# Layer 3's logits on four row groups, and layers 0 and 2 without fused weights

## The chip, the cores and the metric

The kernel runs on one core of a Trainium2 chip. A core has a matrix engine (TensorE, in the profile PE for its matmuls and PEld for its weight loads), a vector engine (VectorE, DVE), a scalar engine (ScalarE, ACT), a general engine (GpSimd, POOL), and queues that start transfers (SP's and ACT's among them). The metric is the device time of one execution in microseconds, lower being better. A profile of one execution gives each engine's instructions.

## The reference

Sixteen images of 256 channels on a 32 x 32 grid go through four layers; everything is float32. N is the 1024 grid places.

- Layer 0: group norm over 8 groups of 32 channels, then q, k and v by 256 x 256 matrices with biases, `softmax(q^T k / 16)` over 1024 places, the weighted sum of v, an output projection with bias, and the residual.
- Layer 1: mean and maximum over channels, two 3 x 3 convolutions on these maps, a sigmoid, and a product with the image.
- Layer 2: the same attention as layer 0 with other weights.
- Layer 3: attention without a norm, where q and k have only 32 rows:

```
energy = clip(q^T k * 32**-0.5, -10, 10)
out    = v softmax(energy)^T
x      = gamma * out + x
```

## The kernel before, in words

An image lies in the on-chip memory as 128 partitions x 2 channel chunks x 1024 places (`xt`). The constants are `CC` = 2 chunks, `HW` = 1024, `HALF` = 512, `NH` = 2 halves, `NT` = 8 tiles of 128 places, `DQK` = 32.

Before the first image `fuse` (lines 125 to 170) multiplies layer 0's q and k weights into one matrix, and its v and projection weights into another, so that logits are `(W xn)^T xn` and the value product gives the projected result at once; the biases are fused too. Layer 2's fuse is called in the first image's turn (line 442).

`attend` (lines 228 to 298) does layers 0 and 2. `group_norm` makes `xn`: statistics on VectorE, two small TensorE products with `gmat` (lines 181 and 189), the inverse root on GpSimd (line 193), scaling on VectorE (line 201). Then q (line 238, 8 products), `values` (line 214, 16 products of 256 columns), and for each half four row tiles: logits over all 1024 places into a two-bank PSUM tile (line 259), the row maximum on VectorE (267), exponential with row sum on ScalarE (270), reciprocal and scaling on VectorE (272, 273), eight transposes on TensorE (278), and their copies (281, 283). The value products follow (line 288), two groups of eight, each added into `xt` on VectorE (295).

`clipped_attend` (lines 365 to 433) does layer 3. One product per half gives q and k together (line 374: 64 output rows); q goes through VectorE (381), k through ScalarE (384). `values` follows. For each half, four pairs of key tiles: two logits products with 32 contraction rows (line 398) into a two-bank tile of `ps_s`, clip on VectorE (402), exponential in place on ScalarE (403). GpSimd adds the probability tiles (406 to 408), the value products run on TensorE (413), `ones` times the sums gives the denominators (423), VectorE takes the reciprocal (425), scales, adds the image (428, 429), and SP stores (432).

PSUM is in three pools, each with two buffers: `ps_s` (two banks a buffer: all logits), `ps_mm` (one bank: all other products) and `ps_tr` (one bank: transposes and denominators). There are three image buffers (`resp`).

Every `yield` ends a step. Two streams, even and odd images, alternate step by step, the second 8 steps behind (`OFFSET`). The tile framework's scheduler then may move instructions of one engine past each other; the order it settles on is fixed when the program is built, and each engine runs its own list in that order. Buffers are handed out in program order, and a writer waits for the last reader of its buffer.

Of the kernel before, what the change touches and what calls it, by code (L numbers as in the profile page):

```python
# [8 lines left out]
FP = mybir.dt.float32  # L9
AF = mybir.ActivationFunctionType  # L10
ALU = mybir.AluOpType
AX = mybir.AxisListType

P = 128
# [7 lines left out]
GROUP = 32  # L22
DQK = 32
EPS = 1e-5

# [10 lines left out]
def kernel(  # L36
# [39 lines left out]
    nc.scalar.dma_start(w0, w_l0.rearrange("(c p) o -> p c o", p=P))  # L76
    vb = const.tile([P, 1, C], FP, name="vb")
    nc.scalar.dma_start(vb[:, 0, :], v_bias[2:3, :].to_broadcast([P, C]))
    bv = const.tile([P, 2, CC], FP, name="bv")
    nc.scalar.dma_start(bv, v_bias[:2, :].rearrange("l (c p) -> p l c", p=P))  # L80
    sc = const.tile([P, NSCAL], FP, name="sc")
    nc.scalar.dma_start(sc, scal.to_broadcast([P, NSCAL]))
    qkb = const.tile([2 * DQK, 1], FP, name="qkb")
    nc.scalar.dma_start(qkb, qk_bias)
    w2 = const.tile([P, CC, 4 * C], FP, name="w2")
    nc.scalar.dma_start(w2, w_l2.rearrange("(c p) o -> p c o", p=P))
    w3 = const.tile([P, CC, 2 * DQK + C], FP, name="w3")
    nc.scalar.dma_start(w3, w_l3.rearrange("(c p) o -> p c o", p=P))

    ident = const.tile([P, P], FP, name="ident")  # L90
# [19 lines left out]
    def build_toep():  # L110
# [9 lines left out]
        nc.vector.tensor_scalar(neg_b2, sc[:, S_B2 : S_B2 + 1], -1.0, None, ALU.mult)  # L120

    def fuse(w, base, layer, nm):
        fw = const.tile([P, CC, 2 * C], FP, name=f"fw_{nm}")
        fb = const.tile([P, CC, 2], FP, name=f"fb_{nm}")
        nat = work.tile([P, CC, 3 * C], FP, tag="nat", name=f"nat_{nm}", bufs=1)
        for j in range(3):
            for r in range(CC):  # L130
                tr = ps_tr.tile([P, C], FP, tag="tr", name=f"wtr_{nm}_{j}_{r}")
                for c in range(CC):
                    nc.tensor.transpose(
                        tr[:, c * P : (c + 1) * P],
                        w[:, c, j * C + r * P : j * C + (r + 1) * P],
                        ident,
                    )
                nc.vector.tensor_copy(nat[:, r, j * C : (j + 1) * C], tr)
        for i in range(CC):
            ps = ps_mm.tile([P, HALF], FP, tag="mm", name=f"fw_{nm}_{i}")  # L140
            for j in range(2):
                lhs, src, rhs = (0, nat, C) if j == 0 else (2 * C, w, 3 * C)
                for r in range(CC):
                    nc.tensor.matmul(
                        ps[:, j * C : (j + 1) * C],
                        nat[:, r, lhs + i * P : lhs + (i + 1) * P],
                        src[:, r, rhs : rhs + C],
                        start=(r == 0),
                        stop=(r == CC - 1),
                    )  # L150

            nc.vector.tensor_scalar(fw[:, i, :C], ps[:, :C], C**-0.5, None, ALU.mult)
            nc.vector.tensor_copy(fw[:, i, C:], ps[:, C:])
        for i in range(CC):
            ps = ps_mm.tile([P, HALF], FP, tag="mm", name=f"fb_{nm}_{i}")
            for j in range(2):
                src, lhs = (nat, C) if j == 0 else (w, 3 * C)
                for r in range(CC):
                    nc.tensor.matmul(
                        ps[:, j : j + 1],  # L160
                        src[:, r, lhs + i * P : lhs + (i + 1) * P],
                        vec[:, r, base + 2 : base + 3] if j == 0 else bv[:, layer, r : r + 1],
                        start=(r == 0),
                        stop=(r == CC - 1),
                    )
            nc.vector.tensor_scalar(fb[:, i, 0:1], ps[:, 0:1], C**-0.5, None, ALU.mult)
            nc.vector.tensor_tensor(
                fb[:, i, 1:2], ps[:, 1:2], vec[:, i, base + 4 : base + 5], ALU.add
            )
        return fw, fb  # L170

# [34 lines left out]
    def values(src, w, col, bias, nm):  # L206

        vt = qkvp.tile([P, NT, C], FP, tag="vt", name=f"vt_{nm}")
        for t2 in range(NT // 2):
            ps = ps_mm.tile([P, 2, C], FP, tag="mm", name=f"vps_{nm}_{t2}")  # L210
            for i in range(2):
                t = 2 * t2 + i
                for c in range(CC):
                    nc.tensor.matmul(  # L214
                        ps[:, i, :],
                        src[:, c, t * P : (t + 1) * P],
                        w[:, c, col : col + C],
                        start=(c == 0),
                        stop=(c == CC - 1),
                    )  # L220
            dst = vt[:, 2 * t2 : 2 * t2 + 2, :]
            if bias is None:
                nc.vector.tensor_copy(dst, ps)
            else:
                nc.vector.tensor_tensor(dst, ps, bias.to_broadcast([P, 2, C]), ALU.add)
        return vt

    def attend(xt, w, fb, base, nm):

        xn = group_norm(xt, base, base + 1, nm)  # L230
        yield
        q = qkvp.tile([P, CC, HW], FP, tag="q", name=f"q_{nm}")
        for o in range(CC):
            for h in range(NH):
                hs = slice(h * HALF, (h + 1) * HALF)
                ps = ps_mm.tile([P, HALF], FP, tag="mm", name=f"q_{nm}_{o}_{h}")
                for c in range(CC):
                    nc.tensor.matmul(  # L238
                        ps,
                        w[:, c, o * P : (o + 1) * P],  # L240
                        xn[:, c, hs],
                        start=(c == 0),
                        stop=(c == CC - 1),
                    )
                nc.scalar.activation(q[:, o, hs], ps, AF.Identity, bias=fb[:, o, 0:1])
            yield
        vt = values(xn, w, C, None, nm)
        yield

        for h in range(NH):  # L250
            hs = slice(h * HALF, (h + 1) * HALF)
            pt = ptp.tile([P, NT, HALF], FP, tag="pt", name=f"pt_{nm}_{h}")
            for j in range(TPH):
                n0 = (h * TPH + j) * P
                s = ps_s.tile([P, HW], FP, tag="s", name=f"s_{nm}_{h}_{j}")
                for mh in range(NH):
                    ms = slice(mh * HALF, (mh + 1) * HALF)
                    for c in range(CC):
                        nc.tensor.matmul(  # L259
                            s[:, ms],  # L260
                            q[:, c, n0 : n0 + P],
                            xn[:, c, ms],
                            start=(c == 0),
# [10 lines left out]
                for g in range(2):  # L274
# [7 lines left out]
                    else:  # L282
                        nc.scalar.copy(dst, tr)  # L283
                yield
            for c in range(CC):
                ps = ps_mm.tile([P, HALF], FP, tag="mm", name=f"av_{nm}_{h}_{c}")
                for m in range(NT):
# [5 lines left out]
                        stop=(m == NT - 1),  # L293
                    )
                nc.vector.scalar_tensor_tensor(  # L295
                    xt[:, c, hs], ps, fb[:, c, 1:2], xt[:, c, hs], ALU.add, ALU.add
                )
                yield

# [65 lines left out]
    def clipped_attend(xt, b):  # L365


        q = qkvp.tile([DQK, HW], FP, tag="q", name=f"q3_{b}")
        k = qkvp.tile([DQK, HW], FP, tag="k", name=f"k3_{b}")
        for h in range(NH):  # L370
            hs = slice(h * HALF, (h + 1) * HALF)
            ps = ps_mm.tile([P, HALF], FP, tag="mm", name=f"qk3_{b}_{h}")
            for c in range(CC):
                nc.tensor.matmul(  # L374
                    ps[: 2 * DQK, :],
                    w3[:, c, : 2 * DQK],
                    xt[:, c, hs],
                    start=(c == 0),
                    stop=(c == CC - 1),
                )  # L380
            nc.vector.tensor_scalar(
                q[:, hs], ps[:DQK, :], qkb[:DQK], DQK**-0.5, ALU.add, ALU.mult
            )
            nc.scalar.activation(
                k[:, hs], ps[DQK : 2 * DQK, :], AF.Identity, bias=qkb[DQK : 2 * DQK]
            )
        vt = values(xt, w3, 2 * DQK, vb[:, 0:1, :], f"l3_{b}")
        yield

        for h in range(NH):  # L390
            hs = slice(h * HALF, (h + 1) * HALF)

            pt = ptp.tile([P, NT, HALF], FP, tag="pt", name=f"pt3_{b}_{h}")
            for m2 in range(NT // 2):
                s = ps_s.tile([P, 2, HALF], FP, tag="s", name=f"s3_{b}_{h}_{m2}")
                for i in range(2):
                    m = 2 * m2 + i
                    nc.tensor.matmul(  # L398
                        s[:, i, :], k[:, m * P : (m + 1) * P], q[:, hs], start=True, stop=True
                    )  # L400
                e = pt[:, 2 * m2 : 2 * m2 + 2, :]
                nc.vector.tensor_scalar(e, s, -10.0, 10.0, ALU.max, ALU.min)  # L402
                nc.scalar.activation(e, e, AF.Exp)  # L403
                yield
# [29 lines left out]

    fw0, fb0 = fuse(w0, L0_GAMMA, 0, "l0")
    late = []

    def sample(b, xt):
        yield from attend(xt, fw0, fb0, L0_GAMMA, f"l0_{b}")
        if b == 0:  # L440
            build_toep()
            late.extend(fuse(w2, L2_GAMMA, 1, "l2"))
        yield from spatial_gate(xt, f"l1_{b}")
        yield from attend(xt, *late, L2_GAMMA, f"l2_{b}")
        yield from clipped_attend(xt, b)
# [79 lines left out]
```

## Time and profile before

| what | us |
|---|---|
| median of 3 runs | 3787.77 |
| lowest and highest | 3785.66, 3788.89 |
| the profiled execution, its own time | 3787.77 |
| its span, first to last instruction | 3785.9 |
| TensorE busy in the span | 3625.0 |
| weight loads busy | 1831.1 |
| VectorE, ScalarE, GpSimd busy | 1661.3, 701.4, 309.4 |
| line 398 (layer 3 logits) busy, 512 records | 303.9 |

The mean granted TensorE clock is 0.957. In the profile's groups a line reads: line of the kernel, engine, operation, output tile <- input tiles, shapes, count, then busy time in us and mean ns of one, then the idle time of that engine just before, with what ended it. A matmul's own duration includes its passage through the array, so that durations in a sequence overlap; the distance between starts is what one costs in a stream. Digit rows cut the span into 40 slices, and each digit is tenths.

### The profile page before, as it was taken

The numbers are of one execution on the slowest core, as the hardware profiler recorded it, in microseconds if no ns is written. First come the engines' busy times: TensorE is split into PE (matmuls) and PEld (weight loads), VectorE is DVE, ScalarE is ACT, GpSimd is POOL, SyncE is SP. The second block draws the span as 40 slices with busy tenths as digits, with TensorE's granted clock in tenths as the row PEclk, the third lists the DMA queues.
The fourth block names the chain that finished last, engine by engine and source line by source line (L and its number), as shares of the span: only waits on it lengthen the run. The fifth ranks groups of instructions, "written<-read, shape, count | busy, mean of one in ns | idle before, by whom it ended". The sixth has DMA issues, their size and how long they took to land.

```text
span 3785.9 us, 26399 instructions
## 1 busy us (share of the span) xinstructions
PE 3625.0 (96%) x10808; PEld 1831.1 (48%) x10808; DVE 1661.3 (44%) x2544; ACT 701.4 (19%) x1073; POOL 309.4 (8%) x301
## 2 busy tenths in 40 slices
PE   7999899998999989999999999999999999999998
PEld 4554345543555435454455544555445554455543
DVE  5543435434344334453344533445334453344533
ACT  1112112121121111221112211212212121121211
POOL 0000100001000010000100001000110001100011
PEclk9999899998999989999899998999989999899998
DMA  1000000000000000000000000000000000000000
GB/s 63 1 1 0 23 23 0 1 0 22 23 1 1 0 23 23 1 0 6 17 23 1 1 6 20 20 0 0 6 23 17 1 1 6 23 6 0 1 6 17
DMA packets 15943, 38.01 MB, mean 10 GB/s; under 512 B 2512, under 2 KB 3024, under 8 KB 15824
## 3 DMA queue, kind: packets, MB, share of 16 engines
q1 hardware_dynamic: 13824, 33.56, 2.5%
q10 hardware_dynamic: 2000, 2.78, 0.2%
q8 instruction: 85, 1.39, 0.1%
q14 instruction: 34, 0.28, 0.0%
HBM read 19.56 MB, written 16.78 MB: 10 GB/s over the span
## 4 chain that ended last, share of the span: by engine, by line
PE 80%; DVE 12%; ACT 4%; POOL 2%; issue 1%; DMA 0%; ACTq 0%; DVEq 0%; POOLq 0%
PE av_l L288 23%; PE s_l L259 14%; PE av L413 12%; PE vps_l L214 7%; PE q_l L238 7%; PE s L398 5%; PE tr_l L278 5%; DVE nmax_l L267 4%; ACT p_l L270 4%; DVE p_l L273 2%; DVE ri L425 2%; PE sum L423 2%; PE qk L374 2%; POOL dg_l L356 1%; DVE o L429 1%
## 5 line engine op out<-in xcount | busy, mean ns | idle before, releaser
L259 PE MATMUL s_l<-xn_l,q_l 128*128 128x512 f32 x2048 | 940.0, 594 | 0.0
L288 PE MATMUL av_l<-pt_l,vt_l 128*128 128x512 f32 x2048 | 925.1, 602 | 0.0
L288 PEld LDWEIGHTS av_l<-pt_l,vt_l 128*128 128x128 f32 x2048 | 386.8, 193 | 466.4 <-issue 453.1
L259 PEld LDWEIGHTS s_l<-xn_l,q_l 128*128 128x128 f32 x2048 | 373.4, 190 | 388.2 <-issue 359.0
L270 ACT ACTIVATE p_l<-s_l,nmax_l 128x1024 f32<-128x1024 f32 x256 | 285.1, 1114 | 1384.5 <-DVE nmax_l L267 1287.3
L413 PE MATMUL av<-pt,vt_l 128*128 128x512 f32 x1024 | 465.9, 605 | 0.0
L267 DVE TENSOR_REDUCE nmax_l<-s_l 128x1 f32<-128x1024 f32 x256 | 313.0, 1223 | 333.4 <-PE s_l L259 333.4
L295 DVE SCALAR_TENSOR_TENSOR x<-av_l,fb_l,x 128x512 f32<-128x512 f32 x128 | 96.1, 751 | 631.2 <-PE av_l L288 631.2
L398 PE MATMUL s<-q,k 32*128 32x512 f32 x512 | 303.9, 722 | 47.1 <-ACT p_l L270 25.0
L278 PEld LDWEIGHTS tr_l<-ident,p_l 128*128 128x128 f32 x2048 | 242.4, 145 | 166.6 <-issue 129.6
L413 PEld LDWEIGHTS av<-pt,vt_l 128*128 128x128 f32 x1024 | 192.2, 193 | 257.5 <-issue 246.1
L278 PE MATMUL tr_l<-ident,p_l 128*128 128x128 f32 x2048 | 280.7, 280 | 27.3 <-DVE p_l L273 27.0
L238 PE MATMUL q_l<-xn_l,fw_l 128*128 128x512 f32 x512 | 260.6, 663 | 33.6 <-DVE xn_l L201 33.6
L281 DVE COPY pt_l<-tr_l 128x512 f32<-128x512 f32 x256 | 176.6, 690 | 170.7 <-PE tr_l L278 166.2
L403 ACT ACTIVATE pt<-pt 128x1024 f32<-128x1024 f32 x128 | 135.3, 1057 | 552.4 <-DVE pt L402 551.3
L425 DVE RECIPROCAL ri<-sum 128x512 f32<-128x512 f32 x32 | 107.4, 3358 | 287.8 <-PE sum L423 287.8
L283 ACT COPY pt_l<-tr_l 128x512 f32<-128x512 f32 x256 | 149.3, 583 | 434.0 <-PE tr_l L278 433.6
L214 PE MATMUL vps_l<-fw_l,xn_l 128*128 128x256 f32 x1024 | 228.9, 379 | 0.0
L214 PEld LDWEIGHTS vps_l<-fw_l,xn_l 128*128 128x128 f32 x1024 | 193.3, 190 | 39.3 <-issue 15.3
L402 DVE TENSOR_SCALAR pt<-s 128x1024 f32<-128x1024 f32 x128 | 155.8, 1218 | 118.7 <-PE s L398 118.7
L398 PEld LDWEIGHTS s<-q,k 32*128 32x128 f32 x512 | 99.6, 214 | 212.7 <-issue 165.3
L406 POOL TENSOR_TENSOR acc<-pt 128x1024 f32<-128x1024 f32 x32 | 79.3, 2477 | 1482.2 <-ACT pt L403 1482.2
(86 smaller groups left out, 2027.9 us busy)
## 6 DMA issues: line engine op xcount, KB each, us to landing
x<-in_x_dram SPq DMA_DIRECT2D x32, 512.0 KB, 4.6
out_dram<-o SPq DMA_DIRECT2D x64, 256.0 KB, 2.0
w<-in_w_l_dram ACTq DMA_DIRECT2D x2, 1024.0 KB, 8.5
w<-in_w_l_dram ACTq DMA_DIRECT2D x1, 320.0 KB, 6.9
tidx<-in_tap_idx_dram ACTq DMA_DIRECT2D x1, 192.0 KB, 6.0
vb<-in_v_bias_dram ACTq DMA_DIRECT2D x1, 128.0 KB, 10.5
vec<-in_vecs_dram ACTq DMA_DIRECT2D x1, 10.0 KB, 4.2
bv<-in_v_bias_dram ACTq DMA_DIRECT2D x1, 2.0 KB, 11.4
```

The lines of the kernel that those rows point to most:

```text
L214: nc.tensor.matmul(ps[:, i, :], src[:, c, t * P : (t + 1) * P], w[:, c, col : col + C], start=(c == 0), stop=(c == CC - 1),)
L238: nc.tensor.matmul(ps, w[:, c, o * P : (o + 1) * P], xn[:, c, hs], start=(c == 0), stop=(c == CC - 1),)
L259: nc.tensor.matmul(s[:, ms], q[:, c, n0 : n0 + P], xn[:, c, ms], start=(c == 0), stop=(c == CC - 1),)
L267: nc.vector.tensor_reduce(nmax, s, AX.X, ALU.max, negate=True)
L270: nc.scalar.activation(pr, s, AF.Exp, bias=nmax, accum_out=rs)
L278: nc.tensor.transpose(tr[:, i, :], pr[:, m * P : (m + 1) * P], ident)
L281: nc.vector.tensor_copy(dst, tr)
L288: nc.tensor.matmul(ps, vt[:, m, c * P : (c + 1) * P], pt[:, m, :], start=(m == 0), stop=(m == NT - 1),)
L398: nc.tensor.matmul(s[:, i, :], k[:, m * P : (m + 1) * P], q[:, hs], start=True, stop=True)
L402: nc.vector.tensor_scalar(e, s, -10.0, 10.0, ALU.max, ALU.min)
L413: nc.tensor.matmul(av, vt[:, m, c * P : (c + 1) * P], pt[:, m, :], start=(m == 0), stop=(m == NT - 1),)
L425: nc.vector.reciprocal(ri, sm)
```

## The change

Two things change together. In layer 3, the q and k weights are laid out twice (`w3qk`: q, q, k, k), so that one product of 128 output rows gives both twice. VectorE copies q to partitions 0 to 63 and again to 64 to 127; ScalarE puts key tile m on the 32 partitions of group m % 4. Four logits products, each on its own 32 partitions, write four banks, which are both buffers of `ps_s`; two clips and two exponentials follow. Layer 3's steps per image go from 11 to 7.

In layers 0 and 2 `fuse` is gone. k is a projection of its own, v has a bias, the value result is copied to the on-chip memory on ScalarE (`ao`), and a projection follows. An attention's steps go from 16 to 20. q's copy moves from ScalarE to VectorE.

```diff
+RG = P // DQK
-    vb = const.tile([P, 1, C], FP, name="vb")
-    nc.scalar.dma_start(vb[:, 0, :], v_bias[2:3, :].to_broadcast([P, C]))
-    bv = const.tile([P, 2, CC], FP, name="bv")
-    nc.scalar.dma_start(bv, v_bias[:2, :].rearrange("l (c p) -> p l c", p=P))
+    vb = const.tile([P, 3, C], FP, name="vb")
+    for i in range(3):
+        nc.scalar.dma_start(vb[:, i, :], v_bias[i : i + 1, :].to_broadcast([P, C]))
...
+    w3qk = const.tile([P, CC, 2, 2, DQK], FP, name="w3qk")
+    qkb4 = const.tile([P, 1], FP, name="qkb4")
+    for i in range(2):
+        nc.gpsimd.tensor_copy(w3qk[:, :, 0, i, :], w3[:, :, :DQK])
+        nc.gpsimd.tensor_copy(w3qk[:, :, 1, i, :], w3[:, :, DQK : 2 * DQK])
+        for j in range(2):
+            nc.scalar.dma_start(
+                qkb4[(2 * j + i) * DQK : (2 * j + i + 1) * DQK],
+                qk_bias[j * DQK : (j + 1) * DQK, :],
+            )
...
-    def fuse(w, base, layer, nm):
...
-    def attend(xt, w, fb, base, nm):
+    def attend(xt, w, base, bias, nm):
...
+        k = qkvp.tile([P, CC, HW], FP, tag="k", name=f"k_{nm}")
+        for j in range(2 * CC):
+            o = j % CC
...
-                nc.scalar.activation(q[:, o, hs], ps, AF.Identity, bias=fb[:, o, 0:1])
+                if j < CC:
+                    nc.vector.tensor_scalar(
+                        q[:, o, hs], ps, vec[:, o, base + 2 : base + 3], C**-0.5, ALU.add, ALU.mult
+                    )
+                else:
+                    nc.scalar.activation(
+                        k[:, o, hs], ps, AF.Identity, bias=vec[:, o, base + 3 : base + 4]
+                    )
             yield
-        vt = values(xn, w, C, None, nm)
+        vt = values(xn, w, 2 * C, bias, nm)
...
-                            xn[:, c, ms],
+                            k[:, c, ms],
...
+            ao = work.tile([P, CC, HALF], FP, tag="ao", name=f"ao_{nm}_{h}")
...
+                nc.scalar.copy(ao[:, c, :], ps)
+                yield
+            for o in range(CC):
+                ps = ps_mm.tile([P, HALF], FP, tag="mm", name=f"pj_{nm}_{h}_{o}")
+                for c in range(CC):
+                    nc.tensor.matmul(
+                        ps,
+                        w[:, c, 3 * C + o * P : 3 * C + (o + 1) * P],
+                        ao[:, c, :],
+                        start=(c == 0),
+                        stop=(c == CC - 1),
+                    )
...
-        q = qkvp.tile([DQK, HW], FP, tag="q", name=f"q3_{b}")
-        k = qkvp.tile([DQK, HW], FP, tag="k", name=f"k3_{b}")
+        q = qkvp.tile([P, HW], FP, tag="q", name=f"q3_{b}")
+        k = qkvp.tile([P, NT // RG, P], FP, tag="k", name=f"k3_{b}")
...
+            for i in range(2):
+                nc.vector.tensor_scalar(
+                    q[i * 64 : (i + 1) * 64, hs], ps[:64, :], qkb4[:64], DQK**-0.5, ALU.add, ALU.mult,
+                )
+            for r in range(RG):
+                src = slice(64 + (r % 2) * DQK, 64 + (r % 2 + 1) * DQK)
+                nc.scalar.activation(
+                    k[r * DQK : (r + 1) * DQK, h, :], ps[src, r * P : (r + 1) * P],
+                    AF.Identity, bias=qkb4[src],
+                )
...
-            for m2 in range(NT // 2):
-                s = ps_s.tile([P, 2, HALF], FP, tag="s", name=f"s3_{b}_{h}_{m2}")
-                for i in range(2):
-                    m = 2 * m2 + i
-                    nc.tensor.matmul(
-                        s[:, i, :], k[:, m * P : (m + 1) * P], q[:, hs], start=True, stop=True
-                    )
-                e = pt[:, 2 * m2 : 2 * m2 + 2, :]
-                nc.vector.tensor_scalar(e, s, -10.0, 10.0, ALU.max, ALU.min)
-                nc.scalar.activation(e, e, AF.Exp)
+            for g in range(NT // RG):
+                tiles = []
+                for i in range(RG // 2):
+                    s = ps_s.tile([P, 2, HALF], FP, tag="s", name=f"s3_{b}_{h}_{g}_{i}")
+                    tiles.append(s)
+                for r in range(RG):
+                    rows = slice(r * DQK, (r + 1) * DQK)
+                    nc.tensor.matmul(
+                        tiles[r // 2][:, r % 2, :], k[rows, g, :], q[rows, hs], start=True, stop=True
+                    )
+                for i in range(RG // 2):
+                    e = pt[:, RG * g + 2 * i : RG * g + 2 * i + 2, :]
+                    nc.vector.tensor_scalar(e, tiles[i], -10.0, 10.0, ALU.max, ALU.min)
+                    nc.scalar.activation(e, e, AF.Exp)
                 yield
...
-    fw0, fb0 = fuse(w0, L0_GAMMA, 0, "l0")
-    late = []
-        yield from attend(xt, fw0, fb0, L0_GAMMA, f"l0_{b}")
+        yield from attend(xt, w0, L0_GAMMA, 0, f"l0_{b}")
-            late.extend(fuse(w2, L2_GAMMA, 1, "l2"))
-        yield from attend(xt, *late, L2_GAMMA, f"l2_{b}")
+        yield from attend(xt, w2, L2_GAMMA, 1, f"l2_{b}")
```

## The prediction

> **What bounds the kernel now.** I read the page's busy times first, then the groups by line, then TensorE in order of time over one steady period. TensorE (PE) is busy 96% of the span, and no other engine reaches half:
>
> ```profile
> PE 3625.0 (96%) x10808; PEld 1831.1 (48%) x10808; DVE 1661.3 (44%) x2544; ACT 701.4 (19%) x1073; POOL 309.4 (8%) x301
> PEclk9999899998999989999899998999989999899998
> ```
>
> The groups give the unit of cost.
>
> ```profile
> L259 PE MATMUL s_l<-xn_l,q_l 128*128 128x512 f32 x2048 | 940.0, 594 | 0.0
> L288 PE MATMUL av_l<-pt_l,vt_l 128*128 128x512 f32 x2048 | 925.1, 602 | 0.0
> L398 PE MATMUL s<-q,k 32*128 32x512 f32 x512 | 303.9, 722 | 47.1 <-ACT p_l L270 25.0
> L238 PE MATMUL q_l<-xn_l,fw_l 128*128 128x512 f32 x512 | 260.6, 663 | 33.6 <-DVE xn_l L201 33.6
> ```
>
> Line 398 is written 256 times (16 samples x 2 halves x 8 key tiles) and recorded 512 times: each product is two passes, each with its own weight load. The weight loads in the timeline start 0.43 us apart, on 128 rows and on 32 alike. So a 512-column pass costs 0.43 us, a product 0.86 us, and 32 rows save nothing now.
>
> The timeline of TensorE repeats from 1318.78 to 1786.42 us: 467.6 us for two samples, eight times. At 0.43 us per 512-column pass and about 0.108 us per 128 columns, the passes of a pair sum to 426 us (per sample 404 of 512 columns, 96 of 256, 144 transposes, 26 tiny). So 42 us of each period are waits and half-speed clock. Two places hold most of it (start, us, what, and in brackets the idle time before it):
>
> ```profile
> 1318.78 3.60 PE L259 MATMUL s_l<-xn_l,q_l 128*128 128x512 f32 x8
> 1322.31 1.98 PE L398 MATMUL s<-q,k 32*128 32x512 f32 x4
> 1327.41 3.77 PE L398 MATMUL s<-q,k 32*128 32x512 f32 x4 [3.12 <-ACT p_l L270]
> 1331.12 1.97 PE L278 MATMUL tr_l<-ident,p_l 128*128 128x128 f32 x8
> 1333.01 3.78 PE L398 MATMUL s<-q,k 32*128 32x512 f32 x4
> ...
> 1387.03 1.12 PE L398 MATMUL s<-q,k 32*128 32x512 f32 x2 [0.90 <-DVE pt L402]
> 1388.08 0.49 PE L181 MATMUL gm_l<-mv_l,gmat 128*128 128x2 f32 x2
> 1388.50 2.07 PE L398 MATMUL s<-q,k 32*128 32x512 f32 x2
> 1392.91 3.75 PE L398 MATMUL s<-q,k 32*128 32x512 f32 x4 [2.35 <-DVE d_l L185]
> 1396.59 0.59 PE L189 MATMUL gv_l<-d_l,gmat 128*128 128x2 f32 x2
> 1398.83 3.48 PE L423 MATMUL sum<-acc,ones 128*128 128x512 f32 x4 [1.65 <-POOL acc L408]
> 1406.38 9.96 PE L238 MATMUL q_l<-xn_l,fw_l 128*128 128x512 f32 x16 [4.08 <-DVE xn_l L201]
> ```
>
> In the first place a logits buffer is not free, because VectorE is in the 3.36 us reciprocal of line 425; four passes afterwards take 3.77 us instead of 1.98, the clock is halved. With the tail of the cold clock this costs about 9.8 us. In the second, the logits of one sample run beside the group norm of the next, with no dense work to cover either: 33.8 us hold 16 us of passes, a loss of 17.7. Together 27.5; the other 14.5 us are many small waits.
>
> **What the Trainium skill says.** "TensorE: Matmul & The Clock Gate", Part 3: products on different row groups run concurrently (four with 32 rows and 512 columns 3.07 times as fast), and matmuls stay in program order in start and end. This trace has only one row group and cannot show either. Part 1 of that page: after an idle window of about 3.4 us the clock halves; here it is halved after 3.12 us. "TensorEngine Tiling (Array Packing)", PSUM Bottleneck: tiling does not speed the emptying of PSUM; line 402 takes 1.22 us per two key tiles whatever TensorE does. "FP8 and Floating Point Precision", TensorE Precision Notes: true FP32 takes four passes; the trace shows two recorded passes, at half the column rate that the first page gives (512 columns in 0.43 us).
>
> **The change, part by part.**
>
> Added products. Without the fused weights each attention has a k projection (8 products more in line 201 of the new kernel) and an output projection (line 272, 8 products). 16 products x 2 passes x 0.43 = 13.8 us; four attentions per period: +55.0 us. They are full-array products on the bounding engine, in sequence with the rest, so all of it counts. Hidden is nothing.
>
> Logits over row groups. If starts are in order, the two passes of one product share a row group and cannot overlap; but the second pass of product r and the first of product r+1 are on different groups and can. A burst of n products then takes n+1 passes instead of 2n. The order in which the changed program's instructions stand on TensorE is not four by four: per sample the first product stands alone (the other three follow after the v products), and in one stream the groups are cut by other products or by the wait for the second buffer. One period: sample A bursts of 1, 3, 2, 2, 2, 2, 2, 2, sample B 1, 3, 4, 4, 2, 2: saving n-1 passes each, 8 + 10 = 18 passes, -7.7 us. Bounds: nothing (0) if float32 passes on different groups do not overlap, below nothing only by a cost per row-group switch, for which entering or leaving 32-row mode gives the nearest row (0.09 us: line 398's first load comes 0.52 us after the pass before it, not 0.43); at the other end every burst in one product's 0.86 us: 36 passes, -15.5 us. I take the middle, because two recorded passes per product in strict order is what the trace and the page together give.
>
> The waits. I worked these through from the new order with the durations of the rows. (1) The same reciprocal is ahead of the row maximum of the other stream's third tile; a logits group now asks for both buffers. The next logits wait about 4.5 us instead of 3.1, then two bursts and a transpose run cold: 24.5 us for 13.8 of work, 10.7 lost (before 9.8). (2) After the row sum of sample A's second half, the other stream's last attention product (line 260 of the new kernel) needs a PSUM bank that is freed by reciprocal and multiply, 3.36 + 0.69 = 4.05 us, and nothing stands between them on TensorE: 4.05 lost, plus about 2.5 for the cold clock. VectorE then stands on the next x (4.6 us to landing, and its statistics 3.1), with the group norm of the coming sample queued behind: another 1.8. With 1.5 of remainder, 10. (3) The second sample's logits now run among the coming sample's k and q projections, 27 us of dense cover; there remain 2.4 us for a clip behind the reciprocal and 1.8 for v copies behind a clip, with 1 for the clock and an occasional wait at the first product: 6 in all. Sum 26.7, against 27.5: -0.8 us. Thus the stall of the second place goes, and new ones nearly fill it.
>
> Emptying. q on VectorE (4 per attention at 0.74 us), a second q copy in layer 3 (0.74), four small k copies on ScalarE (between 0.27, line 349's eight columns, and 0.68, line 384: taken as 0.37), and the output's copy on ScalarE (4 x 0.58): about +110 us VectorE and +100 us ScalarE over the span, to 45% and 20%. They hide under the projection that follows each, 1.72 us of TensorE per bank; without that cover each 0.7 us would be exposed. The v bias adds nothing: line 225 with bias 692 ns, line 223 without 692.
>
> Once only. Layer 0's fuse vanishes: the first q now waits for the group norm, itself behind the scalars' load on VectorE at about 14.4 us and two more broadcast loads ahead of it: q at about 21 instead of 29.8, -9. Layer 2's fuse, -9.5. In the drain the last sample's layer 3 is uncovered by its partner for three steps more: +4. The GpSimd weight copies and the four small bias loads, needed 300 us later, hide behind the first attention; uncovered they would cost about 10 us once.
>
> Sum: 8 x (55.0 - 7.7 - 0.8) = 372, minus 14.5 = +357.5. The profiled execution took 3787.8 us, which is also the median, its span 3785.9: 3785.9 + 357.5 + 1.9 outside the span = 4145 us.
>
> **Rivals.**
>
> No overlap: float32 row groups run one after another. For it: nothing in this trace shows an overlap; against: the skill's figure. 8 x 7.7 = 62 more: 4207 us.
>
> Full overlap: the four products of a burst share one product's time. For it: 3.07 times in the skill; against: two passes per product in order. 8 x 7.8 = 62 less: 4083 us.
>
> Stalls grow: a group holds all logits buffers, the other stream's softmax starves, and the clock stays low. For it: two clips are 2.44 us for 1 to 2 us of logits; against: av products stand behind most groups. At 15 us more per period: 4265 us.
>
> Not slower: the re-timing of the streams removes the waits. One period would have to lose 55.0 - 15.5 - 1.8 (the once-only sum over eight) = 37.7 us of its 42 even with full overlap, in the places named above. Against it is the new bank wait in (2), alone 4.05 plus clock. At that point: 3788 us.
>
> That the change does not reach the array as row groups is the first rival.
>
> **How the numbers follow.** Forecast 0.50, no overlap 0.19, full overlap 0.16, growing stalls 0.13, not slower 0.02. Waits may be off by 8 us per period either way, 64 us: the forecast's own range is 4081 to 4209. With the overlap bounds the range is 4060 to 4235. A difference under 0.2% is about what a measurement of this kernel cannot tell from no change. Slower 0.98, same 0.01, faster 0.01.
>
> **What would show it.** TensorE records: 10808, less the 88 of lines 133, 144 and 159, plus 32 attentions x 32 passes = 11744. Period near 514 us. Within a group, weight loads of neighbouring products at once and a four-product group near 2.2 us warm; 3.5 would mean no overlap, near 0.9 full. At 1382 to 1416's counterpart, logits among q and k products, and after the sum of the first sample's second half an idle TensorE of about 4 us before line 260. The prediction is wrong if the period loses much more or less than 41 us to waits and cold clock, or if a 512-column full-array pass is no longer 0.43.

## The result

The changed kernel takes 4104.22 us, median of four runs (4103.91 to 4106.66); beside it the kernel before took 3786.72 (3785.37 to 3788.89). The ratio is 1.0839, with a 95% interval of 1.0820 to 1.0858. The change costs 317 us; the forecast was 4145, some 41 us too much. The profiled execution took 4103.91 us, its span 4102.1, at a mean granted clock of 0.972 (before: 0.957).

Busy times and clock on the changed kernel's page:

```profile
PE 3883.5 (95%) x11744; PEld 1971.1 (48%) x11744; DVE 1722.2 (42%) x2676; ACT 792.3 (19%) x1297; POOL 305.7 (7%) x305
PEclk9999999999999999999999999999999999999998
```

TensorE is still the bound, with 11744 records as forecast. The dips to 8 in the clock row of before are gone. The changed kernel spends less of its span at the halved clock (called cold from here on), and is slower all the same: the passes themselves are more. The groups by shape:

```profile
L230 PE MATMUL s_l<-k_l,q_l 128*128 128x512 f32 x2048 | 947.0, 601 | 43.2 <-DVE pt L407 34.6
L260 PE MATMUL av_l<-pt_l,vt_l 128*128 128x512 f32 x2048 | 924.8, 604 | 33.7 <-DVE o L433 33.4
L272 PE MATMUL pj_l<-ao_l,w 128*128 128x512 f32 x512 | 233.5, 594 | 0.0
L402 PE MATMUL s<-q,k 32*128 32x512 f32 x512 | 136.3, 675 | 60.6 <-ACT p_l L241 50.4 <-ACT k L382 5.3 <-DVE pt L407 4.8
```

Line 230 was line 259, line 260 was 288, line 402 was 398. A pass is one recorded product of TensorE, so a float32 product is two passes. Three things are to be seen. The products over the row groups are as many as before, but their busy time is the time in which at least one of them runs, and it fell from 303.9 to 136.3 us: they overlap. The output projection of line 272 is new, and nothing of it is hidden. And lines 230 and 260, with no idle time ahead of them before, now have 77 us of it, behind clips (`pt` L407) and the multiply by the reciprocal (`o` L433). The largest wait of before, line 238's 33.6 us for `xn_l`, has no successor: line 201 waits 2.5 us for it.

In order of time TensorE repeats with every pair of images. The period read here is 508.07 us, from a row-sum product of line 428 at 2041.88 to the same one of the next pair at 2549.95; five periods from 1024.80 on average 508.5. From that period and the 20 us before it, start, length, what, and in brackets the idle time before it and what ended it:

```profile
2022.79 1.14 PE L402 MATMUL s<-q,k 32*128 32x512 f32 x8
...
2048.29 2.07 PE L230 MATMUL s_l<-k_l,q_l 128*128 128x512 f32 x2 [3.46 <-DVE pt L407]
2050.15 5.50 PE L174 MATMUL vps_l<-w,xn_l 128*128 128x256 f32 x16
...
2416.49 3.70 PE L230 MATMUL s_l<-k_l,q_l 128*128 128x512 f32 x8 [1.30 <-DVE pt L407]
...
2447.17 1.13 PE L402 MATMUL s<-q,k 32*128 32x512 f32 x4
2452.27 2.08 PE L402 MATMUL s<-q,k 32*128 32x512 f32 x4 [3.98 <-ACT p_l L241]
...
2486.96 1.88 PE L428 MATMUL sum<-acc,ones 128*128 128x512 f32 x4
2493.02 8.83 PE L260 MATMUL av_l<-pt_l,vt_l 128*128 128x512 f32 x16 [4.18 <-DVE o L433]
...
2502.80 0.38 PE L149 MATMUL gv_l<-d_l,gmat 128*128 128x2 f32 x2 [0.84 <-DVE d_l L147]
```

Eight passes over the row groups take 1.14 us, where before they took 3.69 (line 398 at 1363.15); four take 1.13. The three stalls of the prediction are all here: 3.98 us of idle time ahead of the logits behind the reciprocal, 4.18 ahead of line 260, and 3.46 ahead of line 230 for a clip. VectorE's timeline shows that this clip, too, stands behind the reciprocal:

```profile
2043.80 3.36 DVE L430 RECIPROCAL ri<-sum 128x512 f32<-128x512 f32 x1 [17.47 <-PE sum L428]
2047.07 1.16 DVE L407 TENSOR_SCALAR pt<-s 128x1024 f32<-128x1024 f32 x1
```

Around 2022.79 the second sample's logits run among projections without a stall: the place at 1387 to 1406 of the kernel before is gone.

Inside one burst, line 402 alone, in stretches of 0.05 us (stretch; TensorE's busy time and in brackets how many of its records are in progress or begin; the same for weight loads; then granted clock, DMA share and GB/s):

```profile
2022.85:2022.90 0.05, 0.05 (x4) 0.05 (x5) 1.00 0.00 0
2023.35:2023.40 0.05, 0.05 (x8) 0.00 (x0) 1.00 0.00 0
2023.60:2023.65 0.05, 0.05 (x4) 0.00 (x0) 1.00 0.00 0
```

Four passes run at once, near 2023.35 all four change over, and four more run. That fits four products abreast, each taking its own two passes in turn on its own row group; e4 below tests it.

### The profile page after: what moved, and what is told of

Read it like the earlier page. It is cut to its first block, busy times and chain, and to the rows that moved or that the text cites. A ratio compares the mean times of both kernels' runs of the same rounds, so it can differ in the third digit from the quotient of the medians.

```text
span 4102.1 us, 28744 instructions
## 1 busy us (share of the span) xinstructions
PE 3883.5 (95%) x11744; PEld 1971.1 (48%) x11744; DVE 1722.2 (42%) x2676; ACT 792.3 (19%) x1297; POOL 305.7 (7%) x305
## 4 chain that ended last, share of the span: by engine, by line
PE 76%; DVE 11%; issue 7%; ACT 4%; POOL 1%; DMA 0%; ACTq 0%; DVEq 0%; POOLq 0%
PE av_l L260 19%; PE s_l L230 13%; PE qk_l L201 11%; PE vps_l L174 8%; PE av L418 8%; PE tr_l L249 5%; PE pj_l L272 5%; DVE nmax_l L238 4%; ACT p_l L241 4%; PE s L402 2%; DVE p_l L244 2%; DVE ri L430 2%; PE sum L428 1%; DVE pt L407 1%; PE ctr_l L301 1%
## 5 line engine op out<-in xcount | busy, mean ns | idle before, releaser
L230 PE MATMUL s_l<-k_l,q_l 128*128 128x512 f32 x2048 | 947.0, 601 | 43.2 <-DVE pt L407 34.6
L260 PE MATMUL av_l<-pt_l,vt_l 128*128 128x512 f32 x2048 | 924.8, 604 | 33.7 <-DVE o L433 33.4
L230 PEld LDWEIGHTS s_l<-k_l,q_l 128*128 128x128 f32 x2048 | 375.1, 192 | 431.6 <-issue 359.8
L201 PE MATMUL qk_l<-xn_l,w 128*128 128x512 f32 x1024 | 476.7, 610 | 4.7 <-DVE xn_l L161 2.5
L201 PEld LDWEIGHTS qk_l<-xn_l,w 128*128 128x128 f32 x1024 | 197.3, 196 | 259.1 <-issue 213.4
L430 DVE RECIPROCAL ri<-sum 128x512 f32<-128x512 f32 x32 | 107.4, 3358 | 488.3 <-PE sum L428 488.3
L279 DVE SCALAR_TENSOR_TENSOR x<-pj_l,vec,x 128x512 f32<-128x512 f32 x128 | 95.4, 750 | 509.9 <-PE pj_l L272 509.9
L174 PE MATMUL vps_l<-w,xn_l 128*128 128x256 f32 x1024 | 245.2, 395 | 0.0
L272 PE MATMUL pj_l<-ao_l,w 128*128 128x512 f32 x512 | 233.5, 594 | 0.0
L181 DVE TENSOR_TENSOR vt_l<-vps_l,vb 128x512 f32<-128x512 f32 x192 | 132.0, 691 | 219.5 <-PE vps_l L174 219.5
L174 PEld LDWEIGHTS vps_l<-w,xn_l 128*128 128x128 f32 x1024 | 202.0, 200 | 42.6 <-issue 11.7
L210 DVE TENSOR_SCALAR q_l<-qk_l,vec 128x512 f32<-128x512 f32 x128 | 95.9, 750 | 270.9 <-PE qk_l L201 270.8
```

Of the source, the lines that this page charges most:

```text
L174: nc.tensor.matmul(ps[:, i, :], src[:, c, t * P : (t + 1) * P], w[:, c, col : col + C], start=(c == 0), stop=(c == CC - 1),)
L201: nc.tensor.matmul(ps, w[:, c, j * P : (j + 1) * P], xn[:, c, hs], start=(c == 0), stop=(c == CC - 1),)
L230: nc.tensor.matmul(s[:, ms], q[:, c, n0 : n0 + P], k[:, c, ms], start=(c == 0), stop=(c == CC - 1),)
L260: nc.tensor.matmul(ps, vt[:, m, c * P : (c + 1) * P], pt[:, m, :], start=(m == 0), stop=(m == NT - 1),)
L272: nc.tensor.matmul(ps, w[:, c, 3 * C + o * P : 3 * C + (o + 1) * P], ao[:, c, :], start=(c == 0), stop=(c == CC - 1),)
L430: nc.vector.reciprocal(ri, sm)
```

## The experiments

Times are medians of four runs; ratios are to the kernel before, measured beside each of them on the same chip.

### The two parts apart: e1 and e2

The first keeps the fused weights of the kernel before and takes only layer 3's new form from the change (`w3qk`, `qkb4`, q and k on four groups, logits in fours). The second keeps the new projections and takes layer 3 from before.

```diff
 e1, against the kernel before: layer 3 only
+            for g in range(NT // RG):
...
+                        tiles[r // 2][:, r % 2, :], k[rows, g, :], q[rows, hs], start=True, stop=True
 e2, against the changed kernel: layer 3 as before
-            for g in range(NT // RG):
+            for m2 in range(NT // 2):
...
+                        s[:, i, :], k[:, m * P : (m + 1) * P], q[:, hs], start=True, stop=True
```

> The row groups alone, on the kernel before with its fused weights. Theory (a burst of logits products on different groups costs two passes of 0.43 us however many they are): by the new order of instructions each sample has bursts of 1, 3, 4, 4, 2 and 2 products, so 40 passes fewer per pair of samples, 17.2 us, 138 us over eight pairs; with waits about as before 3650 us, and within 60 us of it. Rival (the logits were not what the time went into; clip and softmax waits take their place): 3760 us or more.

> The separate k and output projections alone, layer 3's logits as before. Theory (every added pass counts in full on TensorE): 32 attentions x 32 passes x 0.43 = 440 us, less some 15 us once: 4210 us. Rival (the projections partly fill waits that TensorE had anyway): up to 42 us of waits per pair are there to fill, so 4100 us or less if a third of them is filled.

The kernel before took 3787.07 beside them. e1 took 3654.26 (3653.19 to 3655.12), ratio 0.9649 (0.9635 to 0.9664): layer 3's new form alone, row groups and seven steps together, makes this kernel 133 us faster. Its logits stand on TensorE in 111 unbroken bursts, about 14 per pair of images as in the changed kernel and not the 12 of the expectation, so that 36 passes a period are saved, 15.5 us. Its period is 450.8 us; less 425.8 - 15.5 us of passes, 40.5 are waits and cold clock, nearly as many as before (467.6 less 425.8, 41.8). e2 took 4154.14 (4153.47 to 4160.17), ratio 1.0973 (1.0957 to 1.0989): 367 us for the projections alone. That is neither of the two expectations. Added products come to 55.0 x 8 = 440, less some 14.5 once: the working gives 425, and 58 of it vanished. The period is 515.4, of which 480.8 are passes: waits and cold clock fell from 41.8 to 34.6. e2's groups and its timeline of TensorE, at the counterpart of the second stall of before, show where:

```profile
L378 PE MATMUL s<-q,k 32*128 32x512 f32 x512 | 322.9, 761 | 15.2 <-DVE d_l L136 9.1
```

```profile
1509.78 6.67 PE L378 MATMUL s<-q,k 32*128 32x512 f32 x10
...
1520.27 3.75 PE L378 MATMUL s<-q,k 32*128 32x512 f32 x4 [1.31 <-DVE d_l L136]
```

Each attention has four steps more, so the streams meet at other places. Of the waits of 2.35, 1.65 and 4.08 us in the second stall one of 1.31 is left ahead of the logits, and the next q waits 0.38; the cold clock remains. The first stall went too: line 398's 25.0 us of waiting for `p_l` have no counterpart at line 378. So the two parts do not add: +367 and -133 would be +234, and the change is +317. On top of the projections the row groups gain 50 us instead of 133: 36 passes a period are 124 us, and the waits, which the projections had brought down to 34.6, rise again to 42.8, 66 us over eight periods. What of this is the row groups and what the steps is told apart at the end of this part.

### Whether passes on different row groups overlap: e3 and e4

Both are the changed kernel with every instruction in place, and only the row group of each product is another: all on group 0, or two on 0 and two on 1. The records stand in the same order in the traces of all three on TensorE, VectorE and ScalarE.

```diff
+ROW = (0, 0, 0, 0)              # e4: (0, 0, 1, 1)
...
-        k = qkvp.tile([P, NT // RG, P], FP, tag="k", name=f"k3_{b}")
+        k = qkvp.tile([P, NT, P], FP, tag="k", name=f"k3_{b}")
...
-                    rows = slice(r * DQK, (r + 1) * DQK)
+                    rows = slice(ROW[r] * DQK, (ROW[r] + 1) * DQK)
```

> The changed kernel with all four key tiles and q on row group 0; every engine's instructions stand in the same order as in the changed kernel. Theory (the four groups run at once): a burst of n products takes 2n passes again instead of 2, 36 passes per pair, 15.5 us, 124 us in all, less what the waits for logits buffers take up: 4190 to 4230 us, and an eight-pass burst about 3.6 us instead of 1.1. Rival (the changed order, not the overlap, sets the time): 4104 us.

> The changed kernel with the four products of a group on row groups 0, 0, 1, 1, the order of instructions the same. If each row group works through its own passes and does not wait for the program order across groups, a burst of four products takes four passes, about 1.9 us, and the kernel 24 passes per pair more than the changed one: 4104 + 82 = 4186 us. If passes start in program order across groups, product three can start only with the last pass of product two: seven passes, about 3.2 us, 32 passes per pair more: 4104 + 110 = 4214 us.

e3 took 4191.56 (4186.96 to 4195.71), ratio 1.1071 (1.1053 to 1.1090), e4 4166.79 (4164.02 to 4173.70), ratio 1.1006 (1.0989 to 1.1022). With one group the four products are as long as before; with two, the bursts of three and of four products are equally long. From the timelines of TensorE, e3's and then e4's:

```profile
2063.19 3.69 PE L403 MATMUL s<-q,k 32*128 32x512 f32 x8
```

```profile
2568.42 1.99 PE L403 MATMUL s<-q,k 32*128 32x512 f32 x6
2573.97 1.99 PE L403 MATMUL s<-q,k 32*128 32x512 f32 x8
```

e4 decides how the overlap works. On groups 0, 0, 1, 1 the eight passes stand as 0 0 0 0 1 1 1 1. Passes on one group follow each other, as e3 shows. If a pass also could start only after the start of the one before it, group 1 would begin when group 0 is in its last pass: 7 slots of 0.43 us (a slot is one pass's time), 3.0 us and the 0.2 at the ends. If all first passes stood ahead of all second ones it would be 5 slots, 2.4 us. Measured are 1.99, four slots and the ends. Group 1 starts while group 0 still has passes of earlier products to do. In the changed kernel a burst is two slots whatever its size: 1.07 us of TensorE's stream for four products, as for two. As a whole e4 lies 19 us under the 4186 expected for this case: the burst decides between the two, and the kernel's time is not a sum of bursts.

What of the 36 passes saved per pair comes through as time: 36 x 0.43 x 8 = 124 us by the sum, 87 measured between e3 and the changed kernel. The rest, 37, went into waits: over five periods e3 averages 518.6 us, of which 37.8 are waits and cold clock, the changed kernel 508.5 with 43.2, a difference of 43 over eight periods. What TensorE saves in a burst it can spend again at the next wait. Between e4 and e3 the sum gives 12 passes, 41 us, and 25 were measured.

### The price of the reciprocal: e5 and e6

All three stalls of the changed kernel stand behind VectorE's reciprocal of 128x512. e5 puts a copy in its place in the changed kernel: it leaves the division out and multiplies the output by the sums, and some instructions change their order by it. e6, on e1, lets the row sums come out as 128 partitions x 128 columns instead of 512 columns with every row the same: four blocks of 32 rows, one per 128 query columns. The reciprocal then has a fourth of the columns, and four small products with a constant `gsel` and a copy on ScalarE spread the result again.

```diff
 e5, against the changed kernel
-            nc.vector.reciprocal(ri, sm)
+            nc.vector.tensor_copy(ri, sm)
 e6, against e1
-            for i in range(2):
-                nc.tensor.matmul(sm, ones, acc[:, i, :], start=(i == 0), stop=(i == 1))
+            for j in range(TPH):
+                for i in range(2):
+                    nc.tensor.matmul(
+                        sm[j * GROUP : (j + 1) * GROUP, :P],
+                        ones[:, :GROUP],
+                        acc[:, i, j * P : (j + 1) * P],
...
+            nc.vector.reciprocal(rq, sm[:, :P])
...
+                nc.tensor.matmul(
+                    bc[:, j * P : (j + 1) * P], gsel[:, j, :], rq, start=True, stop=True
+                )
-            nc.vector.reciprocal(ri, sm)
+            nc.scalar.copy(ri, bc)
```

> The changed kernel with a plain copy (about 0.7 us) in place of the 3.36 us reciprocal of layer 3's denominators: the output is multiplied by the sums instead of divided by them. The order of instructions differs in a few places. Theory (the reciprocal, ahead of row maxima, clips and bank releases on VectorE, makes the largest waits of TensorE): waits of 4 to 6 us in each of four places per pair fall by about 2.7 us, and the cold clock behind them mostly goes: 10 to 18 us per pair, so 3960 to 4020 us. Rival (the waits come from holding both logits buffers and from the exponentials, whatever VectorE does first): 4080 us or more.

> Row groups with the fused weights, and the denominators laid out as 4 x 32 partitions by 128 columns, so that VectorE's reciprocal has 128 columns instead of 512; four products of 128 columns spread them again, and ScalarE copies them. The reciprocal should take about 0.9 us. If the reciprocal's length is what holds TensorE up, the waits after a row sum shrink by about 2 us each and the kernel takes 3580 to 3620 us; if the longer chain (product, copy) gives that back, 3640 to 3670 us.

The kernel before took 3785.29 beside them. e5 took 3996.07 (3995.47 to 3996.22), ratio 1.0555 (1.0537 to 1.0573), 108 us under the changed kernel. VectorE's instruction went from 3358 to 692 ns; e5's groups, and then its timeline of TensorE at the counterparts of the three stalls:

```profile
L430 DVE COPY ri<-sum 128x512 f32<-128x512 f32 x32 | 22.1, 692 | 492.9 <-PE sum L428 492.9
```

```profile
1997.51 3.72 PE L174 MATMUL vps_l<-w,xn_l 128*128 128x256 f32 x16 [0.45 <-DVE o L433]
...
2397.00 1.13 PE L402 MATMUL s<-q,k 32*128 32x512 f32 x4 [1.50 <-ACT p_l L241]
2398.06 1.09 PE L249 MATMUL tr_l<-ident,p_l 128*128 128x128 f32 x8
...
2405.14 1.13 PE L402 MATMUL s<-q,k 32*128 32x512 f32 x4 [1.50 <-ACT p_l L241]
2406.20 1.55 PE L249 MATMUL tr_l<-ident,p_l 128*128 128x128 f32 x8
...
2433.22 7.13 PE L260 MATMUL av_l<-pt_l,vt_l 128*128 128x512 f32 x16 [1.51 <-DVE o L433]
```

The waits of 3.98, 4.18 and 3.46 us are 1.50, 1.51 and 0.45, line 260's sixteen passes take 7.13 us instead of 8.83, and by the same sum the period's waits and cold clock are about 29 instead of 42.8. The 32 instructions are 85 us shorter in all, and 108 us are gained: most of the cold clock after these stretches goes with them (the mean granted clock is 0.991, from 0.972). How much of the 108 the changed order of instructions gives or takes is not told apart.

e6 took 3627.97 (3622.55 to 3631.66), ratio 0.9582 (0.9568 to 0.9596). It is the fastest of all kernels here, 26 us under e1, between its two expectations. From its groups, then from its timeline:

```profile
L462 DVE RECIPROCAL rq<-sum 128x128 f32<-128x128 f32 x32 | 30.6, 958 | 309.9 <-PE sum L454 309.9
```

```profile
1752.08 1.13 PE L465 MATMUL bc<-rq,gsel 128*128 128x128 f32 x8 [1.20 <-DVE rq L462]
1754.61 7.13 PE L302 MATMUL av_l<-pt_l,vt_l 128*128 128x512 f32 x16 [1.40 <-DVE o L472]
```

The short reciprocal takes 0.96 us, but the way through TensorE and ScalarE makes a second wait of it (1.20 and 1.40), and the logits of line 427 still wait 2.92 for softmax, at 1828.54. So 2.4 us less of VectorE, 32 times, gave 26 us and not 77. The added products and copy, the waits on the longer chain and the wait that stayed all take from it; e6 doesn't tell their shares apart.

### Groups of four, or fewer steps: e7, e8 and e9

The change also takes layer 3 from 11 steps to 7, since four key tiles share one step. e7 has e1's row groups, but two key tiles at a time in one buffer, and so 11 steps. e8 is e7 with a yield after every second pair. e9 is the kernel before with that yield alone, on one row group.

```diff
 e7, against e1
+            for m2 in range(NT // 2):
+                s = ps_s.tile([P, 2, HALF], FP, tag="s", name=f"s3_{b}_{h}_{m2}")
+                for i in range(2):
+                    m = 2 * m2 + i
+                    rows = slice(m % RG * DQK, (m % RG + 1) * DQK)
...
+                        s[:, i, :], k[rows, m // RG, :], q[rows, hs], start=True, stop=True
 e8, against e7, and e9, against the kernel before
-                yield
+                if m2 % 2:
+                    yield
```

> Row groups with the fused weights, but logits in pairs as before (two products on two groups, one two-bank buffer, eleven steps). If overlap alone counts: a pair costs two passes instead of four, and neighbouring pairs merge, about 35 passes per pair of samples, 15 us: 3665 us. If holding both buffers at once is what leaves waits in the version by fours: 3640 us or less.

> The pairs version with a step after every second pair, so that layer 3 has 7 steps as in the version by fours, while each pair still asks for one buffer only. If the number of steps, that is which work of the other stream stands beside layer 3, is what made the version by fours faster than the pairs: about 3655 us. If it was that neighbouring products by fours overlap more: near the pairs' 3725 us.

> The kernel before with one edit: layer 3 takes 7 steps instead of 11, its logits all on one row group. If the step count moves the second sample's logits away from the coming group norm, up to half of that place's 17.7 us per pair of samples comes back: 3720 to 3750 us. If the steps are worth nothing by themselves: 3787 us, within 8.

e7 took 3725.26 (3723.70 to 3726.47), ratio 0.9840 (0.9825 to 0.9855), missed by both expectations: it gains 60 us, and more than half of e1's gain is gone. Its timeline has the second stall of the kernel before again:

```profile
1826.19 2.07 PE L421 MATMUL s<-q,k 32*128 32x512 f32 x2 [3.46 <-DVE pt L425]
...
1835.59 0.59 PE L199 MATMUL gv_l<-d_l,gmat 128*128 128x2 f32 x2 [1.43 <-DVE d_l L197]
1837.99 3.78 PE L446 MATMUL sum<-acc,ones 128*128 128x512 f32 x4 [1.82 <-POOL acc L431]
1845.86 4.73 PE L248 MATMUL q_l<-xn_l,fw_l 128*128 128x512 f32 x7 [4.08 <-DVE xn_l L211]
```

There the logits are alone with the group norm; passes that are saved turn into idle time. Beside e8 and e9 the kernel before took 3786.56. e8 took 3652.30 (3651.74 to 3653.16), ratio 0.9645 (0.9631 to 0.9659), the same as e1. So the claim on both buffers at once makes no difference between e7 and e1; the number of steps does. It works in two ways. With seven steps the pairs of e8 stand next to each other on TensorE, in 111 bursts like e1's, where e7 has 134: at two slots a burst that is some 20 of the 73 us between e7 and e8. The rest is waits and cold clock. At the same place e8's timeline shows

```profile
1882.70 0.28 PE L191 MATMUL gm_l<-mv_l,gmat 128*128 128x2 f32 x2
...
1885.47 0.28 PE L199 MATMUL gv_l<-d_l,gmat 128*128 128x2 f32 x2
1885.61 7.11 PE L298 MATMUL av_l<-pt_l,vt_l 128*128 128x512 f32 x16
1892.56 7.03 PE L248 MATMUL q_l<-xn_l,fw_l 128*128 128x512 f32 x16
```

no idle time around the group norm, which now stands among value products. e9 took 3765.36 (3762.00 to 3768.78), ratio 0.9946 (0.9930 to 0.9963), between its two expectations: 21 us from the steps alone. Its timeline of TensorE has a wait for the multiply by the reciprocal that the kernel before does not have at that line, and one for the group norm behind it:

```profile
1350.97 8.53 PE L288 MATMUL av_l<-pt_l,vt_l 128*128 128x512 f32 x16 [4.17 <-DVE o L429]
...
1361.50 0.38 PE L189 MATMUL gv_l<-d_l,gmat 128*128 128x2 f32 x2 [1.88 <-DVE d_l L187]
```

So on fused weights the overlap is worth 60 us at 11 steps, the steps 21 without overlap, and both together 134; at 7 steps the overlap thus gives 113.

With the projections the same split comes from e2, e3 and the changed kernel. From e2 to e3, which has 7 steps and no overlap (and the new copies of q and k and the claim on both buffers), the kernel gets 37 us slower; from e3 to the changed kernel the overlap gives 87. That is the gain of 50. The groups of e2 and e3 show what the new form brings:

```profile
L251 PE MATMUL av_l<-pt_l,vt_l 128*128 128x512 f32 x2048 | 915.0, 599 | 0.0
```

```profile
L261 PE MATMUL av_l<-pt_l,vt_l 128*128 128x512 f32 x2048 | 938.2, 611 | 36.3 <-DVE o L434 33.4
```

The wait for the multiply by the reciprocal comes with the seven steps in e3 as in e9, 33.4 us over the span. On fused weights they take the second stall away for it; on the projections most of that stall was gone already. So of the 83 us by which 133 and 50 differ, some 58 lie in the steps and the form around them, and 25 in the overlap.

## Why the prediction came out as it did

The sign and the main term held: the added passes stand in the period in full, and neither the overlap nor the waits come near to paying for them. The model of the overlap did not hold. By its own steps:

- **Added products, +55.0 a period.** Held, as passes. The output projection has no idle time and no cover (line 272: 233.5 us), and a 512-column pass on the full array is still 0.43 us (eight passes of line 201 at 2507.04 take 3.70 with the last one's end).
- **Logits over row groups, -7.7 a period.** This step failed, in its size; its bursts of one, two, three and four products are, as far as a count tells, those of the trace (16, 66, 16 and 15 over the span; it had 16, 64, 16 and 16). It said "starts are in order" and took "the middle, because two recorded passes per product in strict order is what the trace and the page together give". The sentence on program order in the Trainium skill, "TensorE: Matmul & The Clock Gate", Part 3, does not hold here between row groups: in e4 the second group's passes run beside earlier passes of the first (1.99 us for eight passes, where that order would need 3.2). The term is the bound at the other end, 36 passes and -15.5. A burst of four products took 3.44 / 1.07 = 3.2 times less than four in sequence, near the 3.07 of the same part of that page. That figure was right to use, and would alone have given the rival of full overlap, to which the forecast gave 0.16. A four-product group was put near 2.2 us, near 0.9 for that rival; it is 1.14. Over the span: -7.8 x 8 = -62 us against the forecast.
- **Waits, -0.8 a period.** Measured: 508.07 less 465.3 us of passes (425.8 + 55.0 - 15.5) is 42.8, against 41.8 before: +1.0, 1.8 off. In it, idle time grew from 17.6 to 23.8 us (467.64 less 450.04 busy, 508.07 less 484.31), and the cold clock's share shrank. The parts: in (1) 3.98 us instead of 4.5, and about 10.8 lost (10.7 said); in (2) 4.18 (4.05 said) and 1.8 for the clock (2.5 said), with 0.84 and 0.31 left of the group norm's 1.8, about 7 for 10; in (3) 3.46 instead of 2.4, with 2.9 of cold clock on what follows it instead of 1, and no wait of 1.8 for copies of v: 6.4 for 6. Some that were not named, such as 1.30 us ahead of line 230 at 2416.49, are in the remainder. That VectorE stands on the next x held as well: its statistics of line 137 idle 4.27 us on the load at 2499.15. Over the span: 1.8 x 8 = +14.
- **Once only, -14.5.** Measured -7.2 (316.2 of span less 8 x 40.43). The first q starts at 20.38 us as said, 9.4 earlier. The rest, +2.2 instead of -5.5, was not divided between layer 2's fuse, the drain and the ends; it also hangs on the period that is read, which varies between 508.0 and 509.3 in this trace. Over the span: +7.
- **Emptying.** Hidden nearly all, as said: VectorE at 42% and ScalarE at 19%, and of TensorE's idle time 5.3 us ahead of line 402 and 3.4 ahead of line 418 wait for copies of k. ScalarE's busy time grew by 91 us (100 said), VectorE's by 61 and not 110.

Sum of the misses: -62 + 14 + 7 = -41, against 4104.2 - 4145 = -41. The measured time lies between forecast and full overlap, nearer the latter, and what the array does is full overlap; the waits and the ends kept the time from 4083. That 41 us of miss were left and not 62 is luck: two smaller errors pointed the other way. Of the rivals, no overlap falls with e3, which is 87 us slower than the changed kernel. Growing stalls fell with the period: 42.8 us instead of 41.8. Not slower needed 37.7 us of waits to vanish. e5 shows how far off that was: with the reciprocal's 2.7 us taken out everywhere, about 29 still remain.

What the prediction did not see is that the parts are tied together by their waits. It took waits per period as a sum for the finished kernel, and that came out near; but priced alone, the projections cost 367 and not 425, and the row groups and their steps on top of them gain only 50, while on fused weights they gain 133. Its reasons for the added products ("all of it counts") would have missed e2 by 58 us.

## What to carry to other kernels

Where a page gives a measured speed-up and a rule that would forbid it, price both and weigh the measured one more; an experiment that changes only the row group, with every instruction in place, settles it. In interleaved streams, a saving in one stage is worth what the wait behind it allows: look at what is beside it in time. Moving a stage by a few steps was worth 73 us here in one kernel (e7 to e8, some 20 of them by longer bursts), and in another cost up to 37 (e2 to e3). Two parts of a change that fill the same idle place do not add.

## What the runs showed of the hardware

Passes of float32 products on different row groups do not keep program order: four products, eight recorded passes, take 1.07 us of TensorE's stream, as two products do, and eight passes on groups 0, 0, 1, 1 take 1.99, against 3.69 on one group. The eight weight loads of such a burst end within 0.31 us, where they stand 0.43 apart on one group. Products that write different rows overlap as well: in e6 sixteen recorded passes of 128 columns, each product writing its own 32 rows, take 0.67 us with their loads, 0.04 each instead of 0.108; in the trace they start in fours, 0.11 to 0.13 us apart. A reciprocal on VectorE grows with its columns, 3358 ns for 512 and 958 for 128, against 692 for a copy of 512. The clock was halved around single idle stretches of 2.92 (e6) to 4.18 us. Of the two stretches of 1.50 us in e5 shown above, the first was not followed by it (eight transposes take 1.09 us), and the second, 8 us later, was (1.55). The length of one stretch alone does not decide it; what else does, no run here shows.
